# A graph layer's edge gathers: single-row copies taken out, gathers counted by slot, two longer steps per block

## The chip, the cores and the metric

The kernel runs on one core of one Trainium2 chip. The metric is the device time of one execution in microseconds (us), and a kernel's time is the median of several runs. TensorE is called PE (its weight loads PEld), VectorE DVE, ScalarE ACT, GpSimd POOL and SyncE SP. SP and ACT issue plain DMAs from their own queues, and POOL issues the indirect ones (gathers).

## The reference, cut to what matters

```python
src, dst = (edge_index[0], edge_index[1])          # 1,650,000 edges, sorted by dst; 50,000 nodes
Xs = X[src]
m_data = Xs @ W_data.T + b_data
m_ctrl = Xs @ W_control.T + b_control
msg = jnp.where((edge_types == 0)[:, None], m_data, m_ctrl)
agg = jax.ops.segment_sum(msg, dst, num_segments=X.shape[0])
out = relu(agg + (X @ W_self.T + b_self))
x = layernorm(x + out)                             # rows of 128 float32
```

Each node has one edge to itself (a loop) and 32 others on average. The sum over edges comes first in the kernel and the weights after it: for every node it sums the source rows of each edge type, counts the edges of each type for the biases, and multiplies the sums by the weights.

## The kernel before, in words

**Blocks and steps.** The sorted edges are cut into 435 blocks (`NBLK`) of 3,800 edges (`BE`). A block is 28 chunks (`C`) of 128 edges, in four steps (`Q`) of seven (`R`), with 22 fillers (`F`) behind each step and 128 further edges (`X`) at the block's end. The first block has only chunks, and the last has only what is left over.

**A chunk.** POOL gathers 128 source rows with one indirect DMA (`products`, line 451) into one of 70 buffers of the tile `y`. DVE has made a table of ones and zeros two blocks ahead (`onehot`, line 396): each edge's row has a one at its destination's place in the step's window of `W` = 38 nodes, in one of two halves, for the two edge types. PE multiplies the rows by it (line 454) and adds up the chunks of a step in PSUM. `counts` (lines 406 and 411) adds up the table over the chunks of a step, and two small matmuls (line 457) bring the counts into the same PSUM tile. Float32 matmuls appear as two records each.

**A step's end.** `add` (line 465) adds the step's tile into the block's sums at a place read from memory.

**Fillers.** Where a chunk holds a loop, its row would only be the node's own. `fill` therefore puts a filler edge into a loop's place, five blocks ahead (`RAHEAD`): it ranks the loops of a step (the matmuls of lines 256 and 258), compares ranks with 22 numbers (line 307), picks the filler's source and column (lines 310 to 319: the result `idx` is what POOL gathers by) and notes which node's loop was put out (lines 323 and 326). `left_out_columns`, `left_out_matrix` and `left_out_numbers` turn those notes into a number per node, and `left_out_rows` (line 358) multiplies it by the nodes' own rows, which a block loads anyway. `add_left_out` (line 363) adds that to the sums.

**Single rows.** The block's last 128 edges aren't gathered by POOL. `single_rows` copies each row with a DMA of its own: 64 from SP's queue and 64 from ACT's, 16 of each at a time, with addresses loaded into registers first (line 434, issue at line 439). They go two blocks ahead, in turns after each of the four steps. `offsets` (line 425) makes the byte addresses. The rows form a 29th chunk, which PE multiplies in step 3.

**A block's end.** `take_over` (line 470, ACT's only copy in a block) copies what the next block shares with this one from one sums tile to the next. `layer` (lines 475 to 478) multiplies the sums by the weights, `moments` (lines 483 to 489) and `store` (lines 495 to 498) do the relu, residual and norm and write 128 rows. `window` (lines 387 and 389) loads a block's own rows in two layouts.

**Order.** Each engine works in the order in which the program lists its instructions (`manual_schedule`); semaphores between them come from the framework, which also gives gathers a rotating set of eight semaphores. The main loop (lines 520 to 566) lists, for block b: the last `add` of block b-1, `take_over`, `add_left_out`; then for each step `products`, with `layer`, `moments` and `onehot` behind step 0, `store` and `counts` behind step 1, `columns` (once in ten blocks), `left_out_rows` and `fill` behind step 2, `left_out_matrix` and `offsets` behind step 3, and after each step a turn of `single_rows`. So on ACT a block's `take_over` comes after the row issues of the block before.

**Checks.** At the end the kernel reads `bad`, which says whether the edges fit: enough loops in each step for its fillers, no column beyond `W`. If it isn't zero, the general path (`general`) computes all anew.

Of the kernel before, what the change touches and what calls it, by code (L numbers as in the profile page):

```python
# [13 lines left out]
I32 = mybir.dt.int32  # L14
U8 = mybir.dt.uint8
AF = mybir.ActivationFunctionType
# [6 lines left out]
N = 50000  # L23
D = 128
ROW = 4 * D
E = 1650000
# [6 lines left out]

R = 7
W = 38
Q = 4
B = 128
C = R * Q
X = 128
C1 = C + 1  # L40
F = 22
BE = C * CH + Q * F + X
NBLK = 2 + (E - C * CH) // BE
# [5 lines left out]
GROUPS = -(-NBLK // GB)  # L49
GC = GB * C1  # L50
AHEAD = 2
RAHEAD = 5
LOOP = 1024.0

# [24 lines left out]

def straight(ctx, tc, c, x, x_t, src_t, dst_t, etype_t, src_f, dst_f, etype_f, src_x, dst_first, first_p, out):  # L80


# [16 lines left out]
    ohp = ctx.enter_context(tc.tile_pool(name="ohp", bufs=AHEAD + 1))  # L99
    gat = ctx.enter_context(tc.tile_pool(name="gat", bufs=70))  # L100
    fil = ctx.enter_context(tc.tile_pool(name="fil", bufs=2))
# [47 lines left out]

    one_g = {}  # L150

    def load_edges(g):
        t = eds.tile([1, GB * X], I32, name="one_g")
        nc.sync.dma_start(t, src_x[None, g * GB * X:(g + 1) * GB * X])
        one_g[g] = t
        loads[g] = {}
        for name, a in (("s", src_t), ("d", dst_t), ("t", etype_t)):
            t = eds.tile([P, GB, C1], I32, name=name, bufs=1)
            nc.sync.dma_start(t.rearrange("p b c -> p (b c)"), a[:, g * GC:(g + 1) * GC])
            loads[g][name] = t  # L160
        for name, a in (("sf", src_f), ("df", dst_f), ("tf", etype_f)):
            t = eds.tile([GS, F], I32, name=name, bufs=1)
            nc.sync.dma_start(t, a[g * GS:(g + 1) * GS, :])
            loads[g][name] = t
# [69 lines left out]
    def columns(g):  # L234
# [5 lines left out]
        def first_of(rel, d):  # L240
            yield (rel[:, :, :C].rearrange(steps, r=R), d[:, :, :C].rearrange(steps, r=R),
                   first[:, :, :, None].to_broadcast([P, GB, Q, R]))
            yield rel[:, :, C:], d[:, :, C:], first[:, :, Q - 1:]

        def first_of_f(rel, d):
# [5 lines left out]
        nc.vector.memset(h, 0.0)  # L251
        nc.vector.tensor_tensor(h[:, :, :, :R], a["s"][:, :, :C].rearrange(steps, r=R),
                                a["d"][:, :, :C].rearrange(steps, r=R), op=ALU.is_equal)
        rank = ps_r.tile([P, GB * Q, R + 1], F32, name="rank")
# [13 lines left out]
        cb = eds.tile([P, GB, C], F32, name="cb")  # L268
        nc.vector.tensor_scalar(cb, a["t"][:, :, :C], 0.0, float(P), op0=ALU.not_equal, op1=ALU.mult)
        nc.vector.tensor_tensor(cb, cb, a["d"][:, :, :C], op=ALU.add)  # L270
        nc.vector.tensor_tensor(cb, cb, base[:, g * GB:(g + 1) * GB, :].to_broadcast([P, GB, C]), op=ALU.subtract)
# [9 lines left out]
        stay = eds.tile([P, GB, C], F32, name="stay")  # L281
        nc.vector.scalar_tensor_tensor(stay, rk, F - LOOP, v[:, :, :C], op0=ALU.is_ge, op1=ALU.mult)
        col_g[g], rk_g[g], stay_g[g], cb_g[g], vp_g[g] = col, rk, stay, cb, v_f
# [13 lines left out]
    def fill(b):  # L297
# [20 lines left out]
        nc.vector.tensor_single_scalar(idx, vi, 7, op=ALU.logical_shift_right)  # L318
        nc.vector.scalar_tensor_tensor(col_g[g][:, i, :C], idx, -float(P), vi, op0=ALU.mult, op1=ALU.add)
        idxs[b] = idx  # L320
# [44 lines left out]
    def chunks_of(b, q):  # L365

        n = C1 if not plain(b) else C if b == 0 else RCH if b < NBLK else 0
        return range(q * R, max(q * R, min((q + 1) * R if q < Q - 1 else C1, n)))

    def steps_of(b):  # L370
        return [q for q in range(Q) if len(chunks_of(b, q))]

    idxs = {0: idx0}
    bys, pcs, zs, pls = {}, {}, {}, {}
    ats = {}
    ohs, cnts, ys, accs, xws, xTs, pos, hs, mvs, sds = {}, {}, {}, {}, {}, {}, {}, {}, {}, {}

# [4 lines left out]
    def window(b):  # L384
        at = base_of(b)
        xw = stp.tile([B, D], F32, name="xw", bufs=5)
        nc.sync.dma_start(xw, x[bass.ds(at, B), :])
        xT = stp.tile([P, B], F32, name="xT", bufs=5)
        nc.sync.dma_start(xT, x_t[:, bass.ds(at, B)])
        xws[b], xTs[b] = xw, xT  # L390

    def onehot(b):
        g, i = divmod(b, GB)
        n = C1 if not plain(b) else C if b == 0 else RCH
        oh = ohp.tile([P, C1, 2 * W], F32, name="oh")
        nc.vector.tensor_tensor(oh[:, :n, :], col_g[g][:, i, :n, None].to_broadcast([P, n, 2 * W]),  # L396
                                num_ps[:, None, :].to_broadcast([P, n, 2 * W]), op=ALU.is_equal)
        ohs[b] = oh

    def counts(b):  # L400

        cnt = ohp.tile([P, Q, 2 * W], BF16, name="cnt")
        with nc.allow_low_precision(reason="whole numbers up to R + 1"):
            whole = [q for q in range(Q) if len(chunks_of(b, q)) == R]
# [9 lines left out]

    SHARE = X // 2
    TURN = SHARE // Q
    RANGE = dict(min_val=0, max_val=(N - 1) * ROW, skip_runtime_bounds_check_because="where a node's row is")
    x_bytes = x.rearrange("n d -> (n d)").bitcast(U8)[None, :]

    def offsets(b):  # L420

        if not plain(b):
            g, i = divmod(b, GB)
            ats[b] = stp.tile([1, X], I32, name="at_x", bufs=AHEAD + 2)
            nc.vector.tensor_scalar(ats[b], one_g[g][:, i * X:(i + 1) * X], float(ROW), None, op0=ALU.mult)

    def single_rows(b, q):

        if q == 0:
            ys[b] = stp.tile([X, D], F32, name="yx", bufs=AHEAD + 2)  # L430
        both = []
        for j, (eng, dma) in enumerate(((SP, nc.sync), (ACT, nc.scalar))):
            at = j * SHARE + q * TURN
            _, rows = nc.values_load_multi_w_load_instructions(  # L434
                ats[b][0:1, at:at + TURN], engines=[eng], **RANGE)
            both.append([(dma, at + k, row) for k, row in enumerate(rows)])
        for pair in zip(*both):
            for dma, k, row in pair:
                dma.dma_start(ys[b][k:k + 1, :].bitcast(U8), x_bytes[:, bass.ds(row, ROW)])  # L439

    def products(b, q):
        g, i = divmod(b, GB)
        acc = ps.tile([P, 3, W], F32, name="acc")
        ks = chunks_of(b, q)
        for k in ks:
            if k == C:
                r, y = X, ys.pop(b)
            else:
                r = LAST if b == NBLK - 1 and k == RCH - 1 else P
                y = gat.tile([P, D], F32, name="y")  # L450
                nc.gpsimd.indirect_dma_start(  # L451
                    out=y[:r], out_offset=None, in_=x,
                    in_offset=bass.IndirectOffsetOnAxis(ap=idxs[b][:r, k:k + 1], axis=0))
            nc.tensor.matmul(acc[:, :2, :].rearrange("p t w -> p (t w)"), y[:r], ohs[b][:r, k, :],  # L454
                             start=k == ks[0], stop=k == ks[-1])
        for t in range(2):
            nc.tensor.matmul(acc[:, 2, :], to_row[:, t, :], cnts[b][:, q, t * W:(t + 1) * W],  # L457
                             start=t == 0, stop=t == 1)
        accs[b, q] = acc

# [31 lines left out]
    def store(b):  # L492
# [4 lines left out]
        nc.vector.tensor_scalar(o, hs.pop(b), mv[:, 0:1], rstd, op0=ALU.subtract, op1=ALU.mult)  # L497
        nc.sync.dma_start(out[bass.ds(base_of(b), B), :], o)

    for b in range(1, AHEAD + 1):  # L500
        offsets(b)
    columns(0)
# [6 lines left out]
    for b in range(1, RAHEAD):  # L509
# [3 lines left out]
        if b < AHEAD:  # L513
            onehot(b)
            counts(b)
            for q in range(Q):
                single_rows(b, q)
        if b == 1:
            clear_sums()
    for b in range(NBLK + 1):  # L520
# [13 lines left out]
        if b < NBLK:  # L534
            add_left_out(b)
        qs = steps_of(b)
        for q in range(Q):
            if q in qs:
                products(b, q)
            if q == 0 and b > 0:  # L540
# [3 lines left out]
            if q == 3:  # L544
                left_out_columns(b + RAHEAD)
            if q in qs[:-1]:
                add(b, q)
            if q == 0 and b > 0:
# [13 lines left out]
            if q == 3:  # L562
                left_out_matrix(b + RAHEAD)
                offsets(b + AHEAD + 1)
            if not plain(b + AHEAD):
                single_rows(b + AHEAD, q)

# [251 lines left out]
def gnn_resnorm(  # L819
# [9 lines left out]
    etype_f: bass.AP,  # L829
    src_x: bass.AP,  # L830
    dst_first: bass.AP,
# [38 lines left out]
    with ExitStack() as own:  # L870
        straight(own, tc, c, x, x_t, src_t, dst_t, etype_t, src_f, dst_f, etype_f, src_x,
                 dst_first, first_p, out)
# [56 lines left out]
```

## Time and profile before

| What | Value |
|---|---|
| median of 10 runs | 22227.28 us |
| lowest and highest | 22176.15 and 22261.56 us |
| profiled execution: its time | 22276.5 us |
| profiled execution: its span | 22274.5 us |
| instructions in the trace | 239078 |
| granted TensorE clock | 1.0 |
| HBM traffic over the span | 43 GB/s |
| gathers (line 451) | 12160, 947 ns each in the mean |
| multiplications (line 454), records of gathered chunks | 24320, 422 ns each |

The groups of instructions name line, engine, operation, output and inputs with their shapes, the count, then the busy time in us and the mean ns of one. Matmuls are pipelined, so the distance between starts says more than the length of one. Register loads, branches and DMA issues aren't counted as busy: a queue that does nothing but issue looks idle in the engines' shares. A wait's line names who waited, for whom, how long in all (us), how often, and the longest. Releasers are inferred, "remote" being one that can't be named more closely, and "issue" time in which nothing that the profile shows was waited for.

### The profile page before, as it was taken

How to read it: one execution, taken by the hardware profiler on the slowest of the kernel's cores; microseconds unless marked ns; L12 is line 12 of the kernel's file. 1: busy time of each engine (PE TensorE's matmuls, PEld its weight loads, DVE VectorE, ACT ScalarE, POOL GpSimd, SP SyncE). 2: the span in 40 equal slices, each digit the busy share in tenths (PEclk: the TensorE clock that was granted, in tenths of full speed). 3: DMA queues.
4: the chain of work that ended last, by engine and by line, in shares of the span. 5: the costliest groups of instructions: out<-in, count | busy, mean ns of one | idle time of the engine just before them, and what ended most of it. 6: DMA issues, size and time to landing. Idle time of an engine off the chain costs nothing. (4 is left out here: it accounts for less than half of the span.)

```text
span 22274.5 us, 239078 instructions
## 1 busy us (share of the span) xinstructions
PE 7099.3 (32%) x34233; PEld 6717.2 (30%) x34234; DVE 6964.0 (31%) x12861; ACT 353.7 (2%) x875; POOL 11517.9 (52%) x12170
## 2 busy tenths in 40 slices
PE   2333333333333333333333333333333333333333
PEld 2322333333233233333232233332322233322233
DVE  3333333333333333333333233333332333333232
ACT  0000000000000000000000000000000000000000
POOL 5555555555555555555555555555555555555554
DMA  1111111111111111111111111111111111111111
GB/s 47 44 43 44 43 44 44 44 44 44 43 43 44 43 44 44 44 43 45 43 44 43 43 44 43 45 44 43 44 44 43 43 44 43 44 43 44 43 44 38
DMA packets 724493, 968.72 MB, mean 43 GB/s; under 512 B 282786, under 2 KB 522533, under 8 KB 722896
## 3 DMA queue, kind: packets, MB, share of 16 engines
q0 software_dynamic: 389120, 797.69, 14.2%
q1 hardware_dynamic: 277914, 141.12, 2.4%
q10 hardware_dynamic: 55862, 14.50, 0.3%
q14 instruction: 1314, 10.76, 0.2%
q8 instruction: 283, 4.64, 0.1%
HBM read 923.55 MB, written 28.66 MB: 43 GB/s over the span
## 5 line engine op out<-in xcount | busy, mean ns | idle before, releaser
L451 POOL DMA_INDIRECT y<-in_x,idx x12152 | 11508.8, 947 | 10660.0 <-PE acc L454 5666.0
L454 PE MATMUL acc<-oh,y 128*128 128x76 f32 x24320 | 5524.2, 422 | 14.8 <-issue 12.3
L454 PEld LDWEIGHTS acc<-oh,y 128*128 128x128 f32 x24320 | 5364.6, 332 | 14.4 <-issue 14.2
L363 DVE TENSOR_TENSOR sums<-pl,sums 128x384 f32<-128x384 f32 x433 | 241.5, 558 | 12953.3 <-ACT sums L470 12932.8
L349 PE MATMUL pl<-z,ones_b 88*128 88x256 bf16 x433 | 170.7, 394 | 10902.3 <-DVE sums L363 10902.3
L349 PEld LDWEIGHTS <-ones_b 88*128 88x128 bf16 x433 | 45.0, 104 | 10972.7 <-DVE sums L363 10972.7
L406 DVE TENSOR_REDUCE cnt<-oh 128x228 bf16<-128x1596 f32 (+2 forms) x435 | 1278.0, 2938 | 0.1
L333 PE MATMUL small<-ones_b,by 128*88 128x1 bf16 x433 | 100.7, 233 | 3221.4 <-DVE by L326 2502.7
L333 PEld LDWEIGHTS <-by 128*88 128x88 bf16 x433 | 64.0, 148 | 3273.7 <-DVE by L326 2542.4
L396 DVE TENSOR_TENSOR oh<-col,small 128x2204 f32<-128x2204 f32 (+2 forms) x435 | 1050.0, 2414 | 0.0
L340 DVE COPY at<-small 88x1 f32<-88x1 f32 x433 | 66.7, 154 | 1845.3 <-PE po L475 954.8
L457 PEld LDWEIGHTS <-to_row 128*128 128x128 bf16 x3476 | 631.1, 193 | 27.8 <-issue 26.7
L326 DVE TENSOR_REDUCE by<-old 128x88 bf16<-128x616 f32 x433 | 577.8, 1334 | 19.7 <-remote 1.9
L476 PE MATMUL po<-bias,sums 3*128 3x128 f32 x870 | 343.9, 496 | 734.0 <-DVE sums L465 431.7
L470 ACT COPY sums<-sums 128x384 f32 x434 | 222.2, 512 | 21125.7 <-DMA yx<-in_x 20491.9
L478 PE MATMUL po<-wmsgT,sums 128*128 128x128 f32 x1740 | 531.5, 461 | 0.0
L465 DVE TENSOR_TENSOR sums<-acc,sums 128x114 f32 x1738 | 471.9, 272 | 177.3 <-remote 39.2
L411 DVE TENSOR_REDUCE cnt<-oh 128x76 bf16<-128x608 f32 x434 | 501.8, 1156 | 0.0
L457 PE MATMUL acc<-cnt,to_row 128*128 128x38 bf16 x3476 | 481.6, 220 | 36.7 <-issue 36.0
L476 PEld LDWEIGHTS po<-bias,sums 3*128 3x128 f32 x870 | 215.7, 306 | 858.1 <-DVE sums L465 485.8
L478 PEld LDWEIGHTS po<-wmsgT,sums 128*128 128x128 f32 x1740 | 403.3, 322 | 97.6 <-issue 97.6
L307 DVE TENSOR_TENSOR m<-rk,small 128x616 f32<-128x616 f32 x433 | 344.6, 796 | 17.1 <-DVE small L305 2.4
(116 smaller groups left out, 4505.5 us busy)
## 6 DMA issues: line engine op xcount, KB each, us to landing
yx<-in_x ACTq DMA_DIRECT2D x27712, 0.5 KB
yx<-in_x SPq DMA_DIRECT2D x27712, 0.5 KB
y<-in_x,idx POOLq DMA_INDIRECT x12152
xw<-in_x SPq DMA_DIRECT2D x435, 64.0 KB
xT<-in_x_t SPq DMA_DIRECT2D x435, 64.0 KB
out<-o SPq DMA_DIRECT2D x435, 64.0 KB
vf_all<-vd SPq DMA_DIRECT2D x44, 440.0 KB
s<-in_src_t SPq DMA_DIRECT2D x44, 145.0 KB
```

What stands on the lines that cost most here:

```text
L307: nc.vector.tensor_tensor(m, rk_g[g][:, i, :, None].to_broadcast([P, C, F]), rank_no_ps[:, None, :].to_broadcast([P, C, F]), op=ALU.is_equal)
L326: nc.vector.tensor_reduce(by, old.rearrange("p (q r) f -> p q f r", r=R), AX.X, ALU.add)
L363: nc.vector.tensor_tensor(part, pls.pop(b)[:, :, :B], part, op=ALU.add)
L396: nc.vector.tensor_tensor(oh[:, :n, :], col_g[g][:, i, :n, None].to_broadcast([P, n, 2 * W]), num_ps[:, None, :].to_broadcast([P, n, 2 * W ...
L406: nc.vector.tensor_reduce(cnt[:, :n, :], ohs[b][:, :n * R, :].rearrange("p (q r) w -> p q w r", r=R), AX.X, ALU.add)
L411: nc.vector.tensor_reduce(cnt[:, q, :], ohs[b][:, k[0]:k[-1] + 1, :].rearrange("p r w -> p w r"), AX.X, ALU.add)
L451: nc.gpsimd.indirect_dma_start(out=y[:r], out_offset=None, in_=x, in_offset=bass.IndirectOffsetOnAxis(ap=idxs[b][:r, k:k + 1], axis=0))
L454: nc.tensor.matmul(acc[:, :2, :].rearrange("p t w -> p (t w)"), y[:r], ohs[b][:r, k, :], start=k == ks[0], stop=k == ks[-1])
L457: nc.tensor.matmul(acc[:, 2, :], to_row[:, t, :], cnts[b][:, q, t * W:(t + 1) * W], start=t == 0, stop=t == 1)
L465: nc.vector.tensor_tensor(part, accs.pop((b, q)), part, op=ALU.add)
L476: nc.tensor.matmul(po, a[0:3, 2, :B], bias, start=False, stop=False)
L478: nc.tensor.matmul(po, a[:, t, :B], c["wmsgT"][:, t * D:(t + 1) * D], start=False, stop=t == 1)
```

## The change

- `X`, `single_rows`, `offsets`, the input `src_x` and the 29th chunk are gone. A block is 28 chunks and the fillers, 3,684 edges.
- Steps have 14 chunks (`R`), there are two per block (`Q`), with 50 fillers each (`F`) and a window of 64 nodes (`W`). `LOOP`, a mark that keeps ranks of loops apart, is doubled.
- The gathers go in passes of seven chunks (`PASS`), four per block. A pass has one slot of ten (`SLOTS`), a tile of seven chunks, and the slot has a semaphore of its own, which each of the seven gathers raises by 16. PE waits for it once, ahead of the pass's multiplications. The framework adds no semaphores to these gathers.
- The main loop goes over the four passes where it went over the four steps, with the other work at the same places. `add` follows a step's last pass.
- `store` uses the base register that `window` loaded, in place of loading it again.

```diff
-R = 7
-W = 38
-Q = 4
+R = 14
+W = 64
+Q = 2
+PASS = 7
 B = 128
 C = R * Q
-X = 128
-C1 = C + 1
-F = 22
-BE = C * CH + Q * F + X
+F = 50
+BE = C * CH + Q * F
...
+SLOTS = 10
...
-LOOP = 1024.0
+LOOP = 2048.0
...
-    gat = ctx.enter_context(tc.tile_pool(name="gat", bufs=70))
+    gat = ctx.enter_context(tc.tile_pool(name="gat", bufs=SLOTS))
...
+    def passes_of(b):
+
+        for p in range(C // PASS):
+            q = p * PASS // R
+            yield q, [k for k in chunks_of(b, q) if k // PASS == p]
...
-    def single_rows(b, q):
-
-        if q == 0:
-            ys[b] = stp.tile([X, D], F32, name="yx", bufs=AHEAD + 2)
-        both = []
-        for j, (eng, dma) in enumerate(((SP, nc.sync), (ACT, nc.scalar))):
-            at = j * SHARE + q * TURN
-            _, rows = nc.values_load_multi_w_load_instructions(
-                ats[b][0:1, at:at + TURN], engines=[eng], **RANGE)
-            both.append([(dma, at + k, row) for k, row in enumerate(rows)])
-        for pair in zip(*both):
-            for dma, k, row in pair:
-                dma.dma_start(ys[b][k:k + 1, :].bitcast(U8), x_bytes[:, bass.ds(row, ROW)])
...
+    landed = [tc.alloc_semaphore(f"landed{i}") for i in range(SLOTS)]
+    seen = [0] * SLOTS
+    pass_no = [0]
+
+    def gathers(b, ks):
+        i = pass_no[0] % SLOTS
+        pass_no[0] += 1
+        y = gat.tile([P, PASS, D], F32, name="y")
         for k in ks:
...
+            r = LAST if b == NBLK - 1 and k == RCH - 1 else P
+            copy = nc.gpsimd.indirect_dma_start(
+                out=y[:r, k % PASS, :], out_offset=None, in_=x,
+                in_offset=bass.IndirectOffsetOnAxis(ap=idxs[b][:r, k:k + 1], axis=0))
+            copy.then_inc(landed[i], 16)
+            tc.no_tile_sem_insts.add(copy.ins.name)
+            tc.add_to_no_dep_group(f"rows{b}_{ks[0]}", copy.ins)
+        seen[i] += 16 * len(ks)
+        wait = nc.tensor.wait_ge(landed[i], seen[i])
+        tc.declare_fence(wait.ins, group=f"rows{b}_{ks[0]}")
+        return y
+
+    def products(b, q, ks):
+        y = gathers(b, ks)
+        of_step = chunks_of(b, q)
+        if ks[0] == of_step[0]:
+            accs[b, q] = ps.tile([P, 3, W], F32, name="acc")
+        acc = accs[b, q]
+        for k in ks:
+            r = LAST if b == NBLK - 1 and k == RCH - 1 else P
+            nc.tensor.matmul(acc[:, :2, :].rearrange("p t w -> p (t w)"), y[:r, k % PASS, :], ohs[b][:r, k, :],
+                             start=k == of_step[0], stop=k == of_step[-1])
+        if ks[-1] == of_step[-1]:
+            for t in range(2):
+                nc.tensor.matmul(acc[:, 2, :], to_row[:, t, :], cnts[b][:, q, t * W:(t + 1) * W],
+                                 start=t == 0, stop=t == 1)
...
-        nc.sync.dma_start(out[bass.ds(base_of(b), B), :], o)
+        nc.sync.dma_start(out[bass.ds(bases.pop(b), B), :], o)
...
-        qs = steps_of(b)
-        for q in range(Q):
-            if q in qs:
-                products(b, q)
+        last = steps_of(b)[-1:]
+        for q, (step, ks) in enumerate(passes_of(b)):
+            if ks:
+                products(b, step, ks)
...
-            if q in qs[:-1]:
-                add(b, q)
+            if ks and step not in last and ks[-1] == chunks_of(b, step)[-1]:
+                add(b, step)
...
-                offsets(b + AHEAD + 1)
-            if not plain(b + AHEAD):
-                single_rows(b + AHEAD, q)
```

## The prediction

> **What bounds the kernel now.** The page comes first, to see whether any engine is full.
>
> ```profile
> PE 7099.3 (32%) x34233; PEld 6717.2 (30%) x34234; DVE 6964.0 (31%) x12861; ACT 353.7 (2%) x875; POOL 11517.9 (52%) x12170
> ...
> yx<-in_x ACTq DMA_DIRECT2D x27712, 0.5 KB
> yx<-in_x SPq DMA_DIRECT2D x27712, 0.5 KB
> y<-in_x,idx POOLq DMA_INDIRECT x12152
> ```
>
> None is: POOL, which issues the gathers, is busy 52%, the rest a third. But the issues part shows 55,424 single-row copies of 0.5 KB on the SP and ACT queues, and issuing isn't counted as busy. So the list of waits is next, read as a ladder.
>
> ```profile
> ACT sums L470 <- DMA yx<-in_x: 20491.9, 419, 174.9
> DVE sums L363 <- ACT sums L470: 12932.8, 432, 41.1
> PEld L349 <- DVE sums L363: 10972.7, 432, 34.8
> ...
> POOL y L451 <- PE acc L454: 5678.4, 1308, 19.7
> POOL y L451 <- issue: 2807.7, 8932, 4.5
> POOL y L451 <- remote: 1540.3, 1338, 6.1
> ```
>
> Columns: total us, times, longest. The one copy that ACT makes per block (L470) waits 20,492 of 22,274 us, ended by row copies; DVE waits for that copy, PE for DVE, POOL for PE. The timeline of ACT over one block says why:
>
> ```profile
> 11005.03 7.38 ACTq L439 DMA_DIRECT2D yx<-in_x  x10
> 11013.24 0.51 ACT L470 COPY sums<-sums 128x384 f32 x1 [44.92 <-DMA yx<-in_x]
> 11015.50 0.30 ACT L489 ACTIVATE sd<-mv,eps 128x1 f32<-128x1 f32 x1 [1.75 <-DVE mv L487]
> 11016.72 48.33 ACTq L439 DMA_DIRECT2D yx<-in_x  x51
> ```
>
> The copy stands in ACT's program order behind 64 row issues, which last all block; 22,274.5 / 435 blocks = 51.2 us. In a 50 us window PE is busy 16.1 and DVE 15.3. So SP's and ACT's row issue sets the block, and POOL stalls because PE frees its buffers late. Counting gathers issued against chunks multiplied in the trace, POOL runs 58 to 69 chunks ahead; 69 is what its 70 buffers allow.
>
> **What POOL can do when left alone.** The timeline of POOL:
>
> ```profile
> 11028.81 0.95 POOL L451 DMA_INDIRECT y<-in_x,idx  x1 [0.30 <-issue]
> 11030.06 0.94 POOL L451 DMA_INDIRECT y<-in_x,idx  x1 [0.30 <-issue]
> 11031.31 0.94 POOL L451 DMA_INDIRECT y<-in_x,idx  x1 [0.30 <-issue]
> ```
>
> 0.945 busy and 0.305 between: 1.25 us a gather. Of 12,159 spacings 10,035 (83%) are that, mean 1.2508; the rest hold 6,983 us of stall, five sixths ended by PE. A gather's last packet lands 2.2 us after its start and one or two are outstanding, so the transfers don't set the 1.25. Gathers 1 to 5, which wait on no semaphore, have the same spacing: it is the issue itself, and counters of one's own won't shorten it.
>
> **The change part by part.**
>
> *Blocks and gathers.* A block took 28 chunks of 128 edges, 4 x 22 fillers and 128 single rows: 3,800 edges. It will take 28 chunks and 2 x 50 fillers: 3,684. (1,650,000 - 3,584) / 3,684 = 446 and a rest of 3,352 edges, 27 chunks: 448 blocks, 447 x 28 + 27 = 12,543 gathers instead of 12,160. That is 383 more, 479 us at 1.2508.
>
> *Single rows removed.* 128 issues a block, the eight register loads (L434, median about 1 us) and `offsets` on DVE (0.21 us) go. SP keeps three 64 KB transfers a block, ACT its copy and root (0.8 us), so the ladder loses its top rung. Also gone: one chunk per block on PE, 2 x 0.213 us.
>
> *Own counters.* They take POOL's waits on completed gathers away and let PE wait once for seven gathers. PE then starts a pass at its seventh landing, up to 6 x 1.25 us later than now for the first chunk; the 70-chunk lead of the buffers hides it all but at the end. A gather waits for a slot used ten passes (88 us) earlier, long free. Behind PE's wait stand `layer` and the left-out matmuls, and DVE waits for those; POOL does not. The price of the 1,338 stalls by "remote": 1,540 - 1,338 x 0.30 = 1,139 us over 12,160 gathers. The trace holds both ends. From gather 70 on, nearly every gather comes with a separate wait instruction, and there these stalls lie. Before it (gathers 13 to 75, 28.65 to 106.59 us) 62 spacings take 77.9 us, 1.257 each, with ACT's rows in flight all the time:
>
> ```profile
> 25.32 100.68 ACTq L439 DMA_DIRECT2D yx<-in_x  x64
> ...
> 0.00:90.00 90.00, 3.55 (x14) 2.08 (x15) 54.01 (x109) 2.09 (x5) 64.07 (x72) 1.00 0.27 72
> ```
>
> In the second line, DVE and POOL are the third and fifth busy times, in us, with their instructions. The new gathers resemble those: no separate wait for six of seven. So I take 1.2508 to 1.257, and keep 1,139 x 12,543 / 12,160 = 1,175 us as the upper end. Below: nothing, by gathers 1 to 5.
>
> *Steps of 14 chunks, 64 columns.* DVE, per block, from the groups by form. The comparison (L396) goes from 2,204 to 3,584 elements; its slope against the 616-element L307 is (2,418 - 796) / 1,588 = 1.021 ns: +1.41. The counts (L406, L411): 532 and 608 elements with 76 outputs cost 1,081 and 1,158, so 1.01 ns an element, and the 1,596-element row then gives 5.2 ns an output and 0.15 fixed; 3,584 elements with 256 outputs cost 5.1 instead of 4.1: +1.0. Three 616-element products (L307, L310, L323) become 1,400: 3 x 0.80 = +2.4. The two reduces of `fill`: +0.79 and +0.87. Two additions (L465) of 192 instead of four of 114: -0.38. `offsets`: -0.21. Sum +5.9; 16.0 (6,964 / 435) becomes 21.9 us. PE: the multiply with 128 columns instead of 76. L478 has 128 columns, and its records start every 213 ns, as L454's do: nothing. Four to_row matmuls fewer, about -0.5. PE stays near 16 us.
>
> *What hides this.* POOL needs 28 x 1.25 = 35.0 us a block; DVE's 21.9 and PE's 16 lie beside it. Their hand-over too: with t = 0 at the landing of a block's last pass, PE ends it at 3, sums are ready at about 5, the next block's pass 0 lands at 8.75, PE multiplies and runs `layer` to 14; DVE then has 21 us of work and a wait of 2 for pass 1: 37, when the next last pass is ready at 38. Once in ten blocks `columns` adds some 9 us; it is made up before the next layer, and POOL has 60 chunks in hand. If that cover were gone, each us of DVE or PE would cost 448 us.
>
> *A rule against it.* The Trainium skill ("SBUF — State Buffer", section "SBUF: two separate sides") says that a DVE instruction in a two-port mode locks GpSimd out of SBUF, so that the descriptors of its DMAs can't be written, and gives 620 ns becoming about 3,100. By it, if it held for all of DVE's work, a block would take 35 + 22 = 57 us. The rows speak otherwise: in the window 0 to 90 above DVE is busy 54 us and POOL still issues; over the run 98% of gathers last 939 to 957 ns. The added work is tensor_tensor with one operand in PSUM and reduces, which the page doesn't count among the two-port forms. I take zero.
>
> *Small.* Group loads are of 140 instead of 145 KB, the broadcast of fillers 500 instead of 440, per ten blocks, beside a DMA share of 17%: nothing. SP loads one register less a block: nothing.
>
> *Sum.* First gather at 8.5; 12,543 x 1.2508 = 15,689; the first dozen's slow start 3.9; after the last gather 2.2 of landing, 3 of PE and the 24.8 that now lie between the last full step's end and the span's end: 30. Span 15,731, with the 2.0 around it 15,733; with 1.257, 15,811. The median of the runs lies 0.22% under the profiled time (22,227.3 to 22,276.5), which gives 15,700 to 15,775. I take 15,740.
>
> **The rivals.**
>
> A (74%): gathers back to back, 15,650 to 16,200.
>
> B (10%): the "remote" stalls come back: they are not due to the waits but to contention. For it: SP and ACT run slow at the same moments. Against it: gathers 13 to 75. 15,740 + 1,175 = 16,915.
>
> C (9%): the hand-over of DVE and PE takes the place of ACT's queue. My 37 against 38 is close, and a block paced by it at 38 to 42 us gives 17.0 to 18.8 ms; say 17,900. Against: the 70-chunk lead.
>
> D (4%), slower: the port lock of the rule above. 57 us x 448 = 25.5 ms. It decides from 49.6 - 35 = 14.6 us of locked time a block, two thirds of DVE's work.
>
> E (2%), the counters don't do what they say: if a fence orders whole passes, each takes 8.75 of issue + 2.2 of landing + 3 of PE = 14 us, four of them 56 us a block, 25.0 ms, slower too. A data check that fails and starts the general path belongs here; with these edges the least number of loops in a step is 50, just the 50 needed, and the largest column 60 of 64.
>
> Within 0.2%, what a measurement here can tell from no change: 1%.
>
> **How the numbers follow.** Faster: A, B, C = 93%; slower: D, E = 6%. The range reaches from 15,640 (A without its rest) to 17,000: all of A, B's middle and the fast edge of C, about 8 in 10.
>
> **What would show it.** POOL's busy share near 12,543 x 0.945 / 15,730 = 75%; waits of POOL on PE near zero; PE's largest wait at the pass, for gathers; DVE near 9.8 ms in all; L454 starts still 213 ns apart; L406 at 5.1 us, L396 at 3.8. I am wrong if gathers last longer than 0.95 under the denser DVE, if their spacing isn't 1.25, or if POOL still waits for PE.

## The result and the profile after

The changed kernel takes 17,953.33 us (median of 8 runs, 17,948.51 to 17,956.12) where the kernel before takes 22,223.33 us beside it (28 runs, 22,176 to 22,274): a ratio of 0.8078, 95% interval 0.8071 to 0.8085. It is faster, as forecast, but 2,213 us over the 15,740 predicted and outside the range. Chips differ here: on the four chips of experiments 1 to 8 and 11 to 16 the kernel before itself took 15,239 to 15,336 us, on the one of experiments 9 and 10 it took 22,199 us again, so each ratio is taken on one chip.

The page of the changed kernel, its engines and its chain of work that ended last:

```profile
PE 6656.2 (37%) x32928; PEld 5893.3 (33%) x32929; DVE 10690.7 (60%) x11406; ACT 364.3 (2%) x901; POOL 11873.1 (66%) x12553
...
issue 35%; DVE 35%; another core or an unknown queue 18%; PE 12%; ACT 1%; DVEq 0%; ACTq 0%; DMA 0%; SPq 0%
```

POOL has its 12,543 gathers, each still 0.946 us, but is busy 66% of 17,952 us and not 75%. So the gathers were not issued back to back. The chain shows no POOL at all: DVE, PE, time in which an engine waited for nothing that the profile shows ("issue"), and releasers that it can't name ("another core or an unknown queue", called "remote" in the waits). The list of waits of the same run (total us, times, longest):

```profile
PEld L324 <- DVE by L317: 5926.4, 357, 19.8
...
POOL y L423 <- issue: 3610.3, 11809, 1.6
...
PE acc L442 <- issue: 2170.1, 2309, 3.2
...
DVE at L331 <- remote: 1931.7, 224, 12.0
DVE h L471 <- remote: 1684.6, 176, 28.4
POOL y L423 <- remote: 1580.8, 469, 6.3
...
POOL y L423 <- PEq L430: 644.9, 181, 5.3
```

The ladder of before (ACT's copy behind the row issues, then DVE, PE, POOL) is gone. In its place DVE waits for results of PE (L331 copies what the matmul L324 made, L471 takes PE's projection), PE waits for DVE at L324, and PE itself idles 2,170 us between products that wait for nothing. POOL's 11,809 short waits are the 0.305 us between gathers; its 469 by "remote", and 181 more put down to PE's queue, are the real stalls, 5.0 us a block. Nearly all are at the first gather of a pass, where a slot must come free (664 of the 731 spacings over 1.3 us). At these stalls POOL is mostly 50 to 63 chunks ahead of PE, so PE doesn't lack rows. The block takes 40.07 us (17,952 / 448) and POOL needs 35.0 of them.

Two stretches show what is slow. First PE alone (start, duration, engine, line, operation; a row of the timeline joins instructions without a gap):

```profile
9613.10 2.34 PE L442 MATMUL acc<-oh,y 128*128 128x128 f32 x10
9615.84 0.37 PE L442 MATMUL acc<-oh,y 128*128 128x128 f32 x1 [0.41 <-issue]
9617.93 0.27 PE L442 MATMUL acc<-oh,y 128*128 128x128 f32 x1 [1.72 <-issue]
9618.64 0.37 PE L442 MATMUL acc<-oh,y 128*128 128x128 f32 x1 [0.44 <-issue]
9619.34 0.37 PE L442 MATMUL acc<-oh,y 128*128 128x128 f32 x1 [0.33 <-issue]
```

Ten records (five products) start 0.21 us apart; then single ones start 2.09, 0.71 and 0.70 us apart, with no wait that the profile shows. Counted over the whole run, PE's weight loads included, 2,454 starts are 0.7 us apart, 745 are 1.4 and 38 are 2.1: together 2,843 us, 6.3 us a block. Second, all engines elsewhere in the run:

```profile
9045.45 0.24 PE L324 MATMUL small<-ones_b,by 128*100 128x1 bf16 x1 [17.06 <-DVE by L317]
...
9051.78 0.16 DVE L331 COPY at<-small 100x1 f32<-100x1 f32 x1 [6.39 <-remote]
9051.96 0.95 POOL L423 DMA_INDIRECT y<-in_x,idx  x1 [4.11 <-remote]
```

PE ended L324 at 9045.69; DVE, which waits for just that, starts 6.1 us later, and in the same 0.2 us POOL gets its slot: two engines go on at one moment, so PE's signals came late for both. The trace's record of semaphores agrees: the three signals of PE's work from 9045.45 to 9049.3 arrive together, at 9051.70, 9051.75 and 9051.90. That is what "remote" hides. (The ends of matmuls are modelled, so the trace can't say whether the work or only its signals were late.) Where the kernels are quick there are few of these steps. Intervals within 0.03 us of 0.7, 1.4 or 2.1 us between the starts of consecutive instructions of an engine, counted alike in four traces (number, and their sum in us; PE with its weight loads):

| | SP | ACT | PE |
|---|---|---|---|
| before, 22.27 ms | 10,704 (9,818) | 6,578 (6,491) | 44 (45) |
| before, 15.33 ms | 235 (186) | 512 (594) | 1 (1) |
| changed, 17.95 ms | 1,195 (1,201) | 0 | 3,237 (2,843) |
| changed, 15.71 ms | 13 (10) | 0 | 3 (5) |

So most of the slow steps sat in SP's and ACT's queues before the change, and sit in PE's after it. SP, with few instructions left, meets them about as often as before: at 1,195 of its 5,641 records, where it was 10,704 of 63,290.

### The profile page after: what moved, and what is told of

The parts are those of the page before. It is cut to its first block, busy times and chain, and to the rows that moved or that the text cites. A ratio compares the mean times of both kernels' runs of the same rounds, so it can differ in the third digit from the quotient of the medians.

```text
span 17952.2 us, 104890 instructions
## 1 busy us (share of the span) xinstructions
PE 6656.2 (37%) x32928; PEld 5893.3 (33%) x32929; DVE 10690.7 (60%) x11406; ACT 364.3 (2%) x901; POOL 11873.1 (66%) x12553
## 4 chain that ended last, share of the span: by engine, by line
issue 35%; DVE 35%; another core or an unknown queue 18%; PE 12%; ACT 1%; DVEq 0%; ACTq 0%; DMA 0%; SPq 0%
DVE cnt L402 11%; PE acc L442 8%; DVE by L317 5%; DVE m L298 3%; DVE v_new L305 3%; DVE new L301 3%; DVE old L314 3%; PE po L466 2%; PE po L464 1%; DVE sums L453 1%; DVE h L471 1%; DVE pl L349 1%; DVE st L473 1%; PE po L463 0%
## 5 line engine op out<-in xcount | busy, mean ns | idle before, releaser
L423 POOL DMA_INDIRECT y<-in_x,idx x12516 | 11846.0, 946 | 6020.3 <-issue 3602.6
L442 PE MATMUL acc<-oh,y 128*128 128x128 f32 x25086 | 5449.2, 377 | 2209.0 <-issue 2170.1
L442 PEld LDWEIGHTS acc<-oh,y 128*128 128x128 f32 x25086 | 4846.3, 282 | 2519.5 <-issue 2508.0
L324 PE MATMUL small<-ones_b,by 128*100 128x1 bf16 x446 | 108.2, 243 | 7266.5 <-DVE by L317 5827.6
L402 DVE TENSOR_REDUCE cnt<-oh 128x256 bf16<-128x3584 f32 x448 | 2753.2, 6146 | 0.1
L324 PEld LDWEIGHTS <-by 128*100 128x100 bf16 x446 | 70.4, 158 | 7387.8 <-DVE by L317 5926.4
L471 DVE SCALAR_TENSOR_TENSOR h<-po,xw 128x128 f32<-128x128 f32 x448 | 130.7, 292 | 3065.0 <-remote 1684.6
L392 DVE TENSOR_TENSOR oh<-col,small 128x3584 f32<-128x3584 f32 x448 | 1726.7, 3854 | 0.0
L331 DVE COPY at<-small 100x1 f32<-100x1 f32 x446 | 70.6, 158 | 2231.1 <-remote 1931.7
L317 DVE TENSOR_REDUCE by<-old 128x100 bf16<-128x1400 f32 x446 | 1226.9, 2751 | 16.5 <-DVE old L314 1.1
L453 DVE TENSOR_TENSOR sums<-acc,sums 128x192 f32 x896 | 319.2, 356 | 1161.6 <-remote 931.3
L298 DVE TENSOR_TENSOR m<-rk,small 128x1400 f32<-128x1400 f32 x446 | 718.8, 1612 | 16.3 <-issue 1.2
L301 DVE TENSOR_TENSOR new<-m,small 128x1400 f32<-128x1400 f32 x446 | 718.7, 1611 | 15.5
L305 DVE TENSOR_REDUCE v_new<-new 128x28 f32<-128x1400 f32 x446 | 718.4, 1611 | 15.5
L314 DVE TENSOR_TENSOR old<-m,small 128x1400 f32<-128x1400 f32 x446 | 715.2, 1604 | 0.0
```

Source lines behind the costliest of these rows:

```text
L298: nc.vector.tensor_tensor(m, rk_g[g][:, i, :, None].to_broadcast([P, C, F]), rank_no_ps[:, None, :].to_broadcast([P, C, F]), op=ALU.is_equal)
L301: nc.vector.tensor_tensor(new.rearrange("p (q r) f -> p q r f", r=R), m.rearrange("p (q r) f -> p q r f", r=R), vf.rearrange("p (q f) -> p ...
L305: nc.vector.tensor_reduce(v, new, AX.X, ALU.add)
L314: nc.vector.tensor_tensor(old, m, cb[:, :, None].to_broadcast([P, C, F]), op=ALU.mult)
L317: nc.vector.tensor_reduce(by, old.rearrange("p (q r) f -> p q f r", r=R), AX.X, ALU.add)
L402: nc.vector.tensor_reduce(cnt[:, :n, :], ohs[b][:, :n * R, :].rearrange("p (q r) w -> p q w r", r=R), AX.X, ALU.add)
```

## The experiments

The theories at the outset. H: the hand-over between DVE and PE costs 40 us a block as the change builds it, on any chip (the prediction's rival C). S: it costs more only because something makes PE's instructions and signals slow at times, and without that POOL is the bound, as predicted. G: the gathers, or the slots they wait for, set the pace.

**1 to 4, on one chip; the kernel before took 15,239.48 us there (3 runs).** The first leaves out 12 of the 28 gathers of a block. Their products stay and take a neighbouring chunk's rows, so the sums in the output lack the left-out rows and the time is that of DVE's and PE's loop with POOL relieved.

```diff
-        for k in ks:
+        some = [k for k in ks if k % PASS % 2 == 0]
+        for k in some:
...
-            nc.tensor.matmul(acc[:, :2, :].rearrange("p t w -> p (t w)"), y[:r, k % PASS, :], ohs[b][:r, k, :],
+            nc.tensor.matmul(acc[:, :2, :].rearrange("p t w -> p (t w)"), y[:r, k % PASS // 2 * 2, :], ohs[b][:r, k, :],
```

> Leaves out 12 of a block's 28 gathers: only the even places of a pass are gathered, and PE multiplies each gathered chunk in the place of the next one too. Theory H (hand-over): the loop in which DVE waits for PE and PE for DVE sets the block at 40 us, 24 us of DVE's work and 16 of its waits for PE's signals; POOL's stalls only follow. Then the time stays at 17,600 to 18,000 us. Theory G (gathers): POOL's 28 x 1.25 = 35.0 us and its 5 us of stall at the first gathers of passes set the block. Then POOL needs 16 x 1.25 = 20 us and the time falls to what DVE needs, below 14,000 us.

Measured: 12,557.79 us, 28.0 us a block. The loop of DVE and PE needs 28 us, not 40, and POOL now waits for it:

```profile
PE small L324 <- DVE by L317: 7371.6, 446, 25.7
POOL y L424 <- PE acc L443: 3810.4, 925, 10.9
POOL y L424 <- issue: 1899.5, 6232, 0.3
```

Of POOL's waits 3,810 us are put down to PE, none to "remote", none beyond 0.3 us to "issue"; PE waits for DVE once in every block. The expectation gave such a time to G, but it shows no more than that the hand-over as built takes 28 us and leaves 7 of POOL's 35. So H falls here; G is taken up in number 10.

The second moves a block's left-out matmul and matrix one pass later, the third gives the gathers 14 slots, the fourth takes the long steps back and keeps the rest of the change.

```diff
+                left_out_columns(b - 1 + RAHEAD)
-            if q == 3:
-                left_out_columns(b + RAHEAD)
...
-SLOTS = 10
+SLOTS = 14
...
-R = 14
-W = 64
-Q = 2
+R = 7
+W = 38
+Q = 4
...
-F = 50
+F = 22
```

> All work is kept; left_out_columns and left_out_matrix of a block move from behind pass 3 to behind pass 0 of the next block (on PE behind layer, on DVE behind onehot). DVE then no longer waits at L331 (2,231 us in all, 5.0 a block), and PE no longer waits for DVE's L317 ahead of pass 0 (5,828 us, 13 a block). H: the loop loses about 5 us of its 40 and meets POOL's 35.0: 15,800 to 16,200 us. G: PE frees slots somewhat earlier, but POOL's own stalls stay: over 17,000 us.

> 14 slots instead of 10, 98 chunks of lead instead of 70, nothing else. H: the lead is not what is short: 17,850 to 18,000 us, as the changed kernel. G: a first gather of a pass finds its slot free 35 us earlier, its stalls go: 15,750 to 16,000 us.

> The changed kernel with the steps of before: 7 chunks, 4 per block, 22 fillers, window of 38 nodes; still no single rows, still own counters and passes of 7. 450 blocks, 12,583 gathers. DVE's work falls from 24 to about 16 us a block. H: loop 16 + 16 = 32 to 34 us, below POOL's 35.0: 12,583 x 1.2508 and the ends give 15,780 us, up to 16,200. G: POOL's stalls don't depend on the step: 450 x 40 us = 18,000 us.

Measured: 15,714.18 us (ratio 1.0312, 1.0282 to 1.0342), 15,711.98 us (1.031, 1.028 to 1.034) and 15,757.0 us (1.034, 1.031 to 1.037). All sit at POOL's floor: 12,543 x 1.2508 = 15,689 and, for the short steps with their 12,583 gathers, 15,739. None could be told from the others, because none touches the bound, and none contained the slow steps of the result. So number 3's time, which was G's by its expectation, says nothing for G. What the three tell is that the kernel before is 3% quicker than all of them on this chip.

**5 to 8, on a second chip; the kernel before took 15,336.43 us (7 runs).** Numbers 5 and 6 are the two kernels unedited. Number 7 is the changed kernel with the own counters alone taken back (70 tiles under the framework's semaphores; the first diff), number 8 the kernel before with the single rows alone taken out (the second; it also has the change in `store`).

```diff
-    gat = ctx.enter_context(tc.tile_pool(name="gat", bufs=SLOTS))
+    gat = ctx.enter_context(tc.tile_pool(name="gat", bufs=70))
...
-            copy.then_inc(landed[i], 16)
-            tc.no_tile_sem_insts.add(copy.ins.name)
-            tc.add_to_no_dep_group(f"rows{b}_{ks[0]}", copy.ins)
...
-        wait = nc.tensor.wait_ge(landed[i], seen[i])
-        tc.declare_fence(wait.ins, group=f"rows{b}_{ks[0]}")
```

```diff
-BE = C * CH + Q * F + X
+BE = C * CH + Q * F
...
-                offsets(b + AHEAD + 1)
-            if not plain(b + AHEAD):
-                single_rows(b + AHEAD, q)
```

> The changed kernel itself, unedited. In the four runs so far the kernel before took 15,239 us beside them, not 22,223, and in none of their profiles did PE's instructions come in steps of 0.7 us, as they do in the profile of 17,952 us. Theory S (steps): the 5 us a block beyond POOL's 35.0 come from such stretches, which a chip has or doesn't have; where the kernel before takes 15,239 us the changed kernel has none and takes 12,543 x 1.2508 and its ends, 15,700 to 15,740 us, which is 1.03 of before. Theory H: the hand-over of DVE and PE costs 40 us a block as the kernel is built, 17,900 us on any chip, and only the edits of the earlier runs (14 slots, left-out work later, short steps) took it away.

> The kernel before, unedited, for its profile where it is quick. S: no stretches in SP's and ACT's queues; POOL back to back, 12,160 x 1.2508 and the ends, 15,240 us; ACT's copy no longer ends last, and single rows take the place of 3 in 100 gathers at no cost. If row issue is long whatever the chip (my reading on record), 64 row issues still fill each block and POOL waits for PE over 5,000 us in all.

> The changed kernel with the own counters alone taken back: a tile per chunk (70), the framework's semaphores on each gather, PE waiting for each. S: where POOL runs back to back the counters hide nothing: 15,700 to 15,750 us, the same as the changed kernel within 0.3%. If the separate waits of gathers stall POOL by themselves, as the 1,139 us priced on record, 16,500 to 16,900 us.

> The kernel before with the single rows alone taken out: steps of 7 chunks, 22 fillers, framework's semaphores; 450 blocks, 12,583 gathers. S: 12,583 x 1.2508 and the ends, 15,740 to 15,790 us, slower than before by 423 gathers, 529 us; the longer steps and 50 fillers then bring 40 gathers, 50 us, back. If single rows cost time on this chip too, it is faster than before.

Measured: the changed kernel 15,716.01 us (15,715.0 to 15,716.54, 4 runs), ratio 1.0251 (1.0227 to 1.0274): slower. The kernel before 15,330.2. Without own counters 15,703.34 (1.0243, 1.0219 to 1.0266), so the counters bring nothing where POOL is the bound (0.08% the other way). Without the rows alone 15,788.86 (1.0299, 1.0275 to 1.0322).

The waits and the chain of number 5:

```profile
PE acc L442 <- PEq L430: 7864.4, 1711, 7.8
...
POOL y L423 <- issue: 3788.5, 12431, 0.3
...
POOL 69%; issue 23%; DVE 3%; PE 3%; DMA 2%; PEld 0%; POOLq 0%; DVEq 0%; PEldq 0%; SPq 0%; ACT 0%; ACTq 0%
```

This is the picture that the prediction drew: PE waits at the pass for gathers (7,864 us, at the counter's wait, L430), POOL's waits on PE's queue come to 5.0 us in all, and the chain is POOL's gathers with the 0.305 us between them. Why the kernel before is quicker here shows in ACT's timeline of number 6:

```profile
7612.60 30.18 ACTq L439 DMA_DIRECT2D yx<-in_x  x64
...
7647.07 31.49 ACTq L439 DMA_DIRECT2D yx<-in_x  x64
```

The 64 row issues of a block take 30 to 31.5 us, 0.48 us a row, where the trace read for the prediction had 51 rows in 48.33 us, 0.95 us a row. (That was a slow stretch: from the first to the last of a block's 64, counted over all blocks, a row took 0.74 us in that trace and 0.49 in this one.) With the copy and the root the queue goes round in 34.5 us (7612.60 to 7647.07), just under POOL's 35. The single rows then ride along unseen, and they spare POOL one gather in 33. The waits of the same run hold a trap:

```profile
ACT sums L470 <- DMA yx<-in_x: 13558.9, 413, 88.7
DVE sums L363 <- ACT sums L470: 7852.6, 433, 25.7
...
POOL y L451 <- issue: 2108.1, 6906, 0.6
POOL y L451 <- PE acc L454: 999.0, 3131, 3.4
```

The ladder that looked like the bound is still there with 13,559 us on top, and costs nothing: 12,043 of POOL's 12,159 spacings are 1.25 us, and what lies over that sums to 60 us. (The 999 us on PE are 3,131 waits of about 0.3, the ordinary gap under another name.)

**9 and 10, on a chip where the kernel before took 22,199.47 us (7 runs).** The changed kernel unedited, and numbers 2 and 3 in one kernel.

```diff
-SLOTS = 10
+SLOTS = 14
...
+                left_out_columns(b - 1 + RAHEAD)
-                left_out_columns(b + RAHEAD)
```

> The changed kernel unedited, on whatever chip this call gets, to read the next run beside. Two cases. (1) No stretches in which an engine's instructions start 0.7, 1.4 or 2.1 us apart: 15,710 to 15,720 us, POOL's gathers back to back at 1.25 us, ratio to the kernel before about 1.025 to 1.03, the kernel before at 15,240 to 15,340. (2) The stretches are there, on PE: about 17,950 us, 40 us a block, 0.81 of a kernel before at about 22,200. A theory that puts the 40 us down to the hand-over as it is built needs case 2 on every chip and has failed twice.

> 14 slots (98 chunks of lead instead of 70), and a block's left-out matmul and matrix moved one pass later. On a chip without the stretches POOL is the bound and neither matters: 15,705 to 15,725 us. On a chip with them the two theories part. If a block is paced by the DVE and PE hand-over with PE's late signals in it, a longer lead of the gathers buys nothing: the loop still takes 39 to 41 us, 17,700 to 18,100 us. If what costs there is POOL's waiting for slots that a stretch of 6 us frees late, 35 us of extra lead covers it: 15,700 to 16,300 us.

Measured: 17,945.94 us (17,944.57 to 17,948.99, 4 runs), ratio 0.8085 (0.8071 to 0.8098), the recorded result over again; and 17,959.99 us (0.8091, 0.8077 to 0.8104). POOL was now mostly 75 to 91 chunks ahead instead of 50 to 63, and it made no difference: G falls, the rows and their slots are not what is late. The waits of number 10:

```profile
PE acc L442 <- issue: 5279.2, 3234, 4.7
...
PE po L464 <- issue: 3122.0, 244, 16.3
DVE sums L453 <- remote: 2680.4, 372, 50.7
...
DVE h L471 <- remote: 2144.1, 233, 20.0
...
POOL y L423 <- PEq L430: 1597.9, 334, 5.4
```

Number 9 had these two:

```profile
DVE at L331 <- remote: 2391.0, 278, 11.9
...
PE acc L442 <- issue: 2095.0, 2138, 3.2
```

The wait at L331, which the move took off the path, has gone from the top rows; as much has come up at L453 and L471, and PE's own idling has grown from 2,095 to 5,279 us. The loop of DVE and PE still takes 40 us. That fits S with the loop as the pacer: late signals anywhere in it count. It leaves one thing unexplained: PE's slow steps went from 3,079 (2,785 us) to 5,362 (5,936 us), and the time stayed within 0.1%. So their sum does not set the 40 us. A limit on how fast PE is given instructions could hold the block at one length while its parts move, and is called rival R below.

**11 to 16.** To tell S from R, the kernels with short steps should run on such a chip: DVE has 16 instead of 24 us of work a block in them, so by S the block falls under POOL's 35 us, by R it stays at 40. (The expectations call S with the loop as the pacer "theory C".) Numbers 11 and 14 are number 8 again, 12, 15 and 16 are number 4, and 13 is number 1 (whose products stay, other than its expectation says). Their edits are shown above.

> The kernel before with its single rows taken out and nothing else (steps of 7 chunks, 22 fillers, 4 a block, the framework's semaphores, 450 blocks, 12,583 gathers). It took 15,789 us where the stretches are absent. If the kernel before runs at about 22,200 us beside it, the stretches are there. Theory C (DVE's work and PE's signals in turn set the block): DVE works only some 16 us a block here, and 16 + 16 of waiting = 32 us lies under POOL's 35, so 15,800 to 16,100 us; then nearly all of the gain on that chip is the removal of the rows, and the longer steps give 2,200 us of it back. Rival R (the stretches cost a fixed share of any program of this shape, whatever DVE does): 40 us a block again, about 17,900 to 18,100 us. If the kernel before runs at 15,240 to 15,340 beside it: 15,790 again, and nothing is told.

> The changed kernel with steps of 7 chunks and 22 fillers, four a block, instead of 14 and 50, two a block; own counters kept. 15,757 us where the stretches are absent. Where they are present: theory C 15,750 to 16,100 us, since DVE has some 6 us less a block; rival R 17,900 to 18,100 us. The run above against this one gives the counters their price under the stretches: theory C within 1%; if PE's one wait for seven gathers is what stretches, this one is slower by 5% or more.

> The changed kernel without 12 of the 28 gathers and their products in a block (left out of the sums, so the output lacks them). 12,558 us, 28.0 us a block, where the stretches are absent: that is the loop of DVE and PE without POOL. Where they are present: theory C, the same loop with PE's late signals in it: the matmuls left out take their 0.7 us steps with them, so 30 to 36 us a block, 13,500 to 16,100 us. If the loop itself is untouched and POOL's gathers are what the stretches slow, 12,550 to 12,700 us. Rival R: 40 us, 17,900 us.

> The kernel before with only its single rows taken out, on another chip. If the kernel before runs at about 22,200 us beside it: theory C (DVE's 16 us of work and PE's late signals in turn) 15,800 to 16,100 us; rival R (a fixed share of any such program) 17,900 to 18,100 us. If the kernel before runs at 15,240 to 15,340 us: 15,790 to 15,800 us again.

> The changed kernel with steps of 7 chunks and 22 fillers, four a block, on another chip. If the kernel before runs at about 22,200 us beside it: theory C (DVE has some 6 us less a block, so its work and PE's late signals in turn take less than POOL's 35 us) 15,750 to 16,100 us; rival R (a fixed share of any such program) 17,900 to 18,100 us. If the kernel before runs at 15,240 to 15,340 us: 15,755 to 15,770 us again.

> As the run before: with the kernel before at about 22,200 us beside it, theory C 15,750 to 16,100 us and rival R 17,900 to 18,100 us; with the kernel before at 15,240 to 15,340 us, 15,755 to 15,790 us and nothing told.

None of the six met a chip with the stretches; the kernel before took 15,296.61 us beside numbers 11 to 13, then 15,303.56, 15,306.77 and 15,287.09. Rows out alone: 15,802.93 (1.0333, 1.0295 to 1.0371) and 15,817.46 (1.0339, 1.0307 to 1.0372). Short steps: 15,769.94 (1.0312, 1.0273 to 1.035), 15,786.06 (1.032, 1.029 to 1.035) and 15,755.57 (1.0309, 1.0264 to 1.0354). Half the gathers: 12,557.16. They are inconclusive on S and R, and confirm POOL's floor, and that the kernel before is quicker there, on four chips.

## Why the prediction was wrong, point by point

**The step that failed** is to have booked the slow row issues on the rows, so that they would go with them, and to have put what remains on PE and in the hand-over at nothing ("PE stays near 16 us", "their hand-over too"). The prediction noticed that "SP and ACT run slow at the same moments", wrote it down for rival B, and then asked only whether POOL suffers. I took the 51 us of rows as what 64 issues cost and the stalls as what waits cost. What the runs show in its place: instructions start in steps of 0.7 us on that chip; before the change these steps made a row cost 0.74 instead of 0.49 us in the mean, and with the rows gone PE has 3,237 of them in place of 44. The block takes 40.07 us instead of POOL's 35.0, and over 448 blocks that is where the 2,213 us lie. How the steps turn into these 5 us is argued and not isolated (S and R).

**The proof by gathers 13 to 75** was misread. The steps were there: in that stretch of the trace before the change 52 of SP's 75 intervals and 47 of ACT's 73 are of 0.7, 1.4 or 2.1 us, and the 64 rows shown for it took 100.68 us. POOL kept its 1.257 us a gather all the same. So the stretch shows that the steps leave POOL's issue alone. It says nothing on PE, which was busy for 3.55 of the first 90 us.

**The rivals.** What happened has B's reason (something slow that was not due to the waits) at C's place and price: DVE works 23.9 us a block and waits 16 for PE, 40 in all, and C said 17,900 us. That this lies within 0.3% of the result is luck. C's mechanism, the hand-over as built, is not it: experiments 1 and 13 measured that loop at 28.0 us, where the prediction had 37. That "37 against 38" counted 8.75 us of waiting for a pass at POOL's pace into it, and made C look like a matter of 1 us. The slack under POOL's 35 was 7 us, and where the stretches were the loop had grown by 12.

The cover that the prediction named, the 70-chunk lead, isn't there where POOL is the bound: counted in number 5's trace POOL is mostly 4 to 8 chunks ahead of PE. What hides the hand-over there is the slack of 7 us. A lead of 50 to 63 chunks came only where the steps were, and didn't help, since PE and DVE were the ones late.

**POOL's floor** was right: 12,543 gathers at 1.2508 us and 42 us around them gave 15,733, and the changed kernel took 15,716 on one quick chip, its two variants with 14 slots and moved work 15,712 and 15,714 on another, all within 0.15%. Also right: next to no wait of POOL on PE there, PE's largest wait at the pass, no lock-out of GpSimd (gathers 0.945 us with DVE busy 68% of the span), no cost of the fences, nothing from the counters themselves.

**The bound of the kernel before** was read rightly for its own trace and wrongly as a property of the code. Where rows cost 0.49 us the kernel before is bound by POOL as well; then the change takes away a free helper and adds 383 gathers x 1.2508 = 479 us, of which 380 to 475 us were measured (15,716 against 15,336, and 15,714, with the left-out work moved, against 15,239). That is a slower end that no rival of mine had; all of mine that were slower needed a new cost, and this one only needs an old one to vanish.

**DVE's sum** was 21.9 us a block and is 23.9. Three rows of its groups, from the recorded run:

```profile
L402 DVE TENSOR_REDUCE cnt<-oh 128x256 bf16<-128x3584 f32 x448 | 2753.2, 6146 | 0.1
...
L392 DVE TENSOR_TENSOR oh<-col,small 128x3584 f32<-128x3584 f32 x448 | 1726.7, 3854 | 0.0
...
L317 DVE TENSOR_REDUCE by<-old 128x100 bf16<-128x1400 f32 x446 | 1226.9, 2751 | 16.5 <-DVE old L314 1.1
```

The comparison (3.85 against 3.8 forecast) and the products (1.61 against 1.6) were right. The two reduces whose elements lie apart were not: 6.15 us against 5.1, and 2.75 against 2.2. My split into 1.01 ns an element and 5.2 ns an output came from two nearly equal shapes; over 3,584 elements the row is 1.72 ns an element. The 2 us lie under POOL's 35 where POOL is the bound; in the 40 us loop, by S, DVE's work is on the path.

**What stays open.** What makes an engine's instructions start in steps of 0.7 us there and not on the four other chips, and whether it is the chip or something else that ran on it at the time: the steps were met in the recorded runs and in numbers 9 and 10 only. The transfers that bring PE its instructions are no slower there (1.03 us in the median, 1.11 in number 5). PE's steps come back block by block, 85 in 100 of them while DVE stands idle (of PE's other starts 53 in 100). S would look like that, since DVE waits for PE; so would a cause that lies in the waiting. Which part of the change brings the 0.808 there was not isolated: the removal of the rows is the only part that takes work off SP and ACT, but it did not run alone on such a chip. And S against R: whether less DVE work a block would bring the changed kernel from 17,950 to about 15,760 there was asked in numbers 11, 12 and 14 to 16, and none of them met such a chip. No version beat both kernels: on four chips the kernel before is the quickest of all that compute the whole result, and where it is slow, the changed kernel is.

## What to carry to other kernels

When several engines go slow at the same moments for no wait of their own, do not book that time on the code that happens to stand there: here it came up again in the engine next on the path, and what it cost was what exceeded that path's slack. A ladder of waits shows who waits for whom, not that the top rung is the bound; price the top rung's operation by its quickest stretches beside its mean before you take it for a cost that a change removes (in the trace before the change a tenth of ACT's turns of 16 rows took 0.43 us a row or less, and a block's 64 took 0.74 in the mean). And a free helper of the bounding engine, here 128 rows a block beside POOL, is given up only after asking what the bound would be if the helper were quick.

## What the runs showed of the hardware that was not expected

One and the same kernel took 22,199 to 22,223 us where the stretches were there and 15,239 to 15,336 on four chips where they were not; the changed kernel 17,946 to 17,953 and 15,716. In the slow stretches instructions start 0.7, 1.4 or 2.1 us apart, and in the row shown PE's signal arrives 6.0 us after the end that the trace gives for its matmul. POOL's gathers are left alone: 1.25 us from start to start with the steps and without.

The granted clock of a page can mislead: the changed kernel shows 0.59 to 0.60 with its products 112 ns apart where the row says full speed and 213 ns where it says half, while the kernel before shows 1.0 and its products start 213 ns apart all through. No change of clock is recorded in that run at all. Its 1.0 was no sign of full speed.
